# Giving all large tiles of a two-layer graph kernel one starting place modulo 256 bytes

## The chip, the cores and the metric

The kernel runs on one core of a Trainium2 chip. The metric is the device time of the whole kernel in microseconds; of several runs the median is taken.

## The reference

The input is x, 128 batches of a 128 x 512 matrix (nodes by features), in float32, and one 128 x 128 matrix adj, most of whose entries are zero. Two layers follow each other:

```python
# layer 0
h = jnp.maximum(_layernorm(x, axis=-1), 0.0)
y = jnp.einsum('nm,bmd->bnd', adj, h)
x = x + jnp.einsum('bnd,do->bno', y, weight) + bias
# layer 1
h = jnp.maximum(_layernorm(x, axis=-1), 0.0)
qkv = (h @ w_qkv)                      # 8 heads of 64
attn = q @ k^T * scale, masked where adj == 0, softmax
o = (attn @ v) @ w_proj + b_proj
x = x + o + layernorm(o) * gamma + beta
```

So each batch has one 128 x 512 by 512 x 512 product in layer 0 and four of them in layer 1 (Q, K, V and the projection), beside the small products with adj and in the attention.

## The kernel before

**Products in three parts.** Almost every large product is done with both factors split into a high and a low part, kept in the type float32r (called fp32r here; `HALF` in the code). Three sums of four matmuls, with 128 x 128 stationary and 128 x 512 moving operands, make one product: high by high, low by low, and the mixed part. `split_weights` (L333) splits the weights into `wA` (the weights of layer 0, and later the projection's), `wqk` and `wv`; `split_left` (L427) splits what comes out of PSUM into three tiles h, l and s. `times_weights` (L435, matmul on L441) does a product with the data as the stationary operand and the weights as the moving one: layer 0 (`wA` with tiles t10 to t13, t24, t25), V (`wv` with `hp`) and the projection (`wA` with t14 to t17). Q and K (L579) are the other way round: `wqk` is stationary, and `hp`, the split and transposed activations of four batches, moves. These are the fp32r products. The products with adj (L482), the scores (L636), the attention (L695) and a few plain products at the two ends (L491, L713) are in float32 and show as two records each.

**Stages.** Layer 0 (`phase1`) runs over the batches, from the fifth in pairs: load x, statistics, normalise and ReLU on ScalarE, mix with adj, split, product, add on VectorE, store twice to DRAM. Layer 1 (`phase2_group`) runs over 32 groups of four batches: fetch, normalise, transpose through DRAM (`exchange`, with `VectorE`'s 32 x 32 transposes on L542 and L677), split into `hp`, Q and K, scores, mask and softmax, V, attention, projection, second norm, store.

**Order.** A planner written in the kernel (`Plan`) gets every step with an engine, a cost, a due time and the buffers that it reads and writes, and simulates the five queues once; the instructions are then emitted in the planned order, and each engine works through its own queue. All DMAs are issued from SP's queue (L266). The planner knows buffers by name alone.

**Places in SBUF.** A tile pool stacks its tiles one after the other, in the order in which they are first made; a later tile of the same tag has the same place. Pools are stacked in the order in which they are opened. Before the change there are two in SBUF: `const` (hp, minus_half, beta_b, wA, some, maskb, means, wqk, wv, bp_b, gamma_b, in this order) and, behind it, `work`, with the t tiles (2048 bytes in each partition), the f tiles (4096 bytes) and the small m, n and l tiles (64 bytes: 16 float32 numbers, for the statistics of a normalisation or of a softmax). minus_half and some have 64 bytes as well; every other tile has a multiple of 512 bytes. The first tile, hp, begins at 128 modulo 256. The small tiles stand between the large ones, and each moves all that follow by 64 bytes. So the tiles that TensorE reads begin at these places modulo 256:

| tile | place modulo 256 |
|---|---|
| hp | 128 |
| wA | 192 |
| wqk, wv | 0 |
| t0 to t4, t8, t16, t20, t11, f0 to f3 | 0 |
| t5 to t7, t17, t9, t12, t13, t18, t19, t23 to t25 | 64 |
| t14, t15, t21, t22 | 128 |
| t10 | 192 |

Slices of these tiles begin a multiple of 512 bytes further on, so a slice has its tile's place modulo 256.

Of the kernel before, what the change touches and what calls it, by code (L numbers as in the profile page):

```python
# [15 lines left out]
P = 128  # L16
# [182 lines left out]
def kernel(  # L199
# [19 lines left out]
    assert N == P and HD * 2 == P and B % 2 == 0  # L219
    scale = HD ** -0.5  # L220

    const = ctx.enter_context(tc.tile_pool(name="const", bufs=1))
    work = ctx.enter_context(tc.tile_pool(name="work", bufs=1))
    dram = ctx.enter_context(tc.tile_pool(name="dram", bufs=B, space=bass.MemoryType.DRAM))
# [28 lines left out]
    def buf(name, shape, dtype=F32):  # L253
        if name == "ps":
            return Buf(G["ps"], lambda tag: psum.tile(shape, dtype, name=tag, tag=tag, bufs=1))
        return Buf(G[name], lambda tag: work.tile(shape, dtype, name=tag, tag=tag, bufs=1))

    def fixed(shape, name, dtype=F32):
        return Buf(None, lambda _: const.tile(shape, dtype, name=name))

    def in_dram(shape, name):
        return Buf(None, lambda _: dram.tile(shape, F32, name=name))
# [15 lines left out]


    bp_b, gamma_b, beta_b = (fixed([P, D], n) for n in ("bp_b", "gamma_b", "beta_b"))  # L280
    b0_b, junk = buf("b0", [P, D]), buf("junk", [P, D])
    adjT, maskb = buf("adjT", [P, P]), fixed([P, P], "maskb")
    minus_half = fixed([P, 16], "minus_half")
    ident = buf("ident", [P, P])
    some = fixed([P, 16], "some")

# [504 lines left out]
```

## Time and profile before

| | |
|---|---|
| median of 3 runs | 2199.84 us (2199.65 to 2200.28) |
| profiled execution | 2199.62 us, of which the span from first to last instruction is 2197.8 |
| granted TensorE clock | 0.999 of full speed |
| busy: TensorE, VectorE, ScalarE, GpSimd | 2182.2, 1717.8, 1482.1, 1524.9 us |
| fp32r matmuls | 7560: 2952 on L441 with wA, 1536 on L441 with wv, 3072 on L579 |
| DMA | 408.09 MB on SP's queue, 59.0% of the 16 engines' span |

In the profile PE is TensorE's matmuls, PEld its weight loads, which run beside them, DVE is VectorE, ACT ScalarE, POOL GpSimd and SP the queue that issues the DMAs. A line number names the line of the kernel that made the instruction. Consecutive matmuls overlap:[...] the sum of durations is more than the time that they hold TensorE, and the distance from one start to the next tells what one costs.

### The profile page before, as it was taken

To read this page: it belongs to the slowest core of one execution; us is meant where nothing else is said; L and a number is where in the kernel's file an instruction comes from. 1 tells how busy PE (TensorE), PEld (TensorE's weight loads), DVE (VectorE), ACT (ScalarE), POOL (GpSimd) and SP (SyncE) were. 2 spreads that over 40 slices of the span, in tenths; PEclk is the share of its full clock that TensorE was granted. 3 is DMA by queue.
4 is the path that set the end of the run, shared out by engine and by line. 5 is a ranking of instruction groups with operands and counts; after the bars stand their busy time and mean duration, and the time that the engine had idled before them with its cause. 6 is when DMAs were issued, how large, how long until landed. Compare 5 with 4: busy or idle time off the path is not lost.

```text
span 2197.8 us, 40584 instructions
## 1 busy us (share of the span) xinstructions
PE 2182.2 (99%) x12811; PEld 1780.3 (81%) x12811; DVE 1717.8 (78%) x3271; ACT 1482.1 (67%) x4238; POOL 1524.9 (69%) x1276
## 2 busy tenths in 40 slices
PE   9999999999999999999999999999999999999998
PEld 7888888888878888888888888888888888888885
DVE  7988887886777777777777777777777777777777
ACT  7887777767666666666666666666666666666653
POOL 6878778784667666666666666666666666666654
PEclk9999999999999999999999999999999999999999
DMA  7766666664556656655555555565555656555553
GB/s 248 237 213 223 216 212 220 227 220 153 170 169 194 183 178 184 183 180 175 173 173 173 173 175 181 178 183 182 187 180 182 186 172 193 173 175 181 176 177 119
DMA packets 297863, 410.69 MB, mean 187 GB/s; under 512 B 33072, under 2 KB 163248, under 8 KB 297648
## 3 DMA queue, kind: packets, MB, share of 16 engines
q1 hardware_dynamic: 297648, 408.09, 59.0%
q8 instruction: 102, 1.67, 0.3%
q14 instruction: 113, 0.93, 0.1%
HBM read 207.68 MB, written 200.28 MB: 186 GB/s over the span
## 4 chain that ended last, share of the span: by engine, by line
PE 92%; DVE 1%; POOL 0%; issue 0%; DMA 0%; ACT 0%; SPq 0%; POOLq 0%; DVEq 0%; ACTq 0%
PE b L441 44%; PE b L579 33%; PE b L636 6%; PE b L695 5%; PE b L482 4%; DMA out_dram<-t 0%; DVE t L729 0%; POOL f L661 0%; DVE t L727 0%; POOL m L383 0%; DVE m L377 0%; DVE t L715 0%; SPq L266 0%; ACT t L538 0%; DVE l L377 0%
## 5 line engine op out<-in xcount | busy, mean ns | idle before, releaser
L441 PE MATMUL b<-wA,t 128*128 128x512 f32 x2952 | 762.7, 397 | 1.8 <-DVE t L430 1.4
L579 PE MATMUL b<-hp,wqk 128*128 128x512 f32 x3072 | 755.9, 396 | 0.8 <-ACT t L586 0.8
L579 PEld LDWEIGHTS b<-hp,wqk 128*128 128x128 f32 x3072 | 575.6, 188 | 140.1 <-issue 4.6
L441 PEld LDWEIGHTS b<-wA,t 128*128 128x128 f32 x2952 | 545.3, 188 | 122.2 <-DVE t L430 2.4
L721 POOL TENSOR_TENSOR t<-t,t 128x512 f32<-128x512 f32 x126 | 163.9, 1301 | 446.7 <-DVE t L452 317.6
L656 ACT ACTIVATE f<-f,n 128x128 f32<-128x128 f32 x1024 | 397.1, 391 | 2.1
L441 PE MATMUL b<-wv,hp 128*128 128x512 f32 x1536 | 394.6, 398 | 0.8 <-DVE t L452 0.8
L441 PEld LDWEIGHTS b<-wv,hp 128*128 128x128 f32 x1536 | 283.6, 188 | 70.8 <-DVE t L452 1.2
L586 ACT ACTIVATE t<-b 128x512 f32<-128x512 f32 x256 | 152.4, 595 | 264.2 <-PE b L579 264.0
L644 DVE TENSOR_TENSOR f<-b,maskb 128x512 f32<-128x512 f32 x256 | 166.4, 683 | 143.4 <-PE b L695 78.3
L661 POOL TENSOR_TENSOR f<-f,n 128x1024 f32<-128x1024 f32 x128 | 245.8, 1920 | 31.4 <-DVE n L660 31.4
L429 ACT ACTIVATE t<-b 128x512 fp32r<-128x512 f32 x246 | 145.2, 590 | 111.3 <-PE b L482 87.7
L587 DVE TENSOR_TENSOR t<-b,t 128x512 f32<-128x512 f32 x256 | 172.8, 675 | 46.0 <-PE b L579 35.7
L546 POOL TENSOR_TENSOR hp<-t,hp 128x512 fp32r<-128x512 f32 x128 | 163.4, 1296 | 57.8 <-ACT hp L545 55.1
L656 ACT ACTIVATION_READ_ACCUMULATOR f<-f,n 128x1 f32 x1024 | 193.6, 189 | 0.0
L430 DVE TENSOR_TENSOR t<-b,t 128x512 fp32r<-128x512 f32 x246 | 166.9, 679 | 24.6 <-ACT t L429 24.2
L431 DVE SCALAR_TENSOR_TENSOR t<-t,b 128x512 fp32r<-128x512 f32 x246 | 166.5, 677 | 0.0
L725 POOL TENSOR_TENSOR t<-t,t 128x512 f32<-128x512 f32 x122 | 158.4, 1299 | 9.5
L549 POOL TENSOR_TENSOR hp<-hp 128x512 fp32r<-128x512 f32 x128 | 163.7, 1299 | 0.6
L724 POOL TENSOR_TENSOR t<-t,gamma_b 128x512 f32<-128x512 f32 x122 | 157.5, 1291 | 9.0 <-ACT t L723 9.0
L677 DVE STREAM_TRANSPOSE f<-f 128x1024 f32<-128x1024 f32 x126 | 155.9, 1237 | 4.0 <-DMA f<-d 3.3
L614 ACT ACTIVATE t<-b 128x512 f32<-128x512 f32 x128 | 75.8, 592 | 120.8 <-PE b L441 120.7
(119 smaller groups left out, 3204.9 us busy)
## 6 DMA issues: line engine op xcount, KB each, us to landing
d<-f SPq DMA_DIRECT2D x126, 512.0 KB, 3.3
f<-d SPq DMA_DIRECT2D x504, 128.0 KB, 4.1
t<-x1d SPq DMA_DIRECT2D x128, 256.0 KB, 4.3
d<-t SPq DMA_DIRECT2D x128, 256.0 KB, 3.0
t<-d SPq DMA_DIRECT2D x512, 64.0 KB, 3.6
t<-x1b SPq DMA_DIRECT2D x128, 256.0 KB, 3.7
out_dram<-t SPq DMA_DIRECT2D x128, 256.0 KB, 3.4
t<-in_x_dram SPq DMA_DIRECT2D x91, 256.0 KB, 3.0
```

Source lines behind the costliest of these rows:

```text
L430: op("DVE", 0.69, lambda: nc.vector.tensor_tensor(l.ap, p.ap, h.ap.bitcast(F32), op=ALU.subtract), r=[p, h], w=[l], what=name + "l")
L431: op("DVE", 0.69, lambda: nc.vector.scalar_tensor_tensor(s.ap, h.ap.bitcast(F32), UP, p.ap, op0=ALU.mult, op1=ALU.subtract), r=[p, h], w=[ ...
L441: nc.tensor.matmul(p.ap, lhsT=parts[m][2]()[:, c], rhs=w.ap[:, m, c, :], start=start and c == 0, stop=stop and c == C - 1)
L546: op("POOL", 1.35, lambda ht=ht, h=h, l=l: nc.gpsimd.tensor_tensor(l(), ht(), h().bitcast(F32), op=ALU.subtract), r=[h1, HP[i, 0]], w=[HP[ ...
L549: op("POOL", 1.38, lambda l=l, s=s: nc.gpsimd.tensor_tensor(s(), s().bitcast(F32), l().bitcast(F32), op=ALU.subtract), r=[HP[i, 1]], w=[HP ...
L579: nc.tensor.matmul(p.ap, lhsT=wqk.ap[:, which, c, col:col + P], rhs=hp[:, pick, :, which, c, :], start=start and c == 0, stop=stop and c = ...
L587: op("DVE", 0.69, lambda r=r, b=b: nc.vector.tensor_tensor(r.ap, b.ap, r.ap, op=ALU.add), r=[b], w=[r], due=tg + (4 if g < 7 else 2), what ...
L644: op("DVE", 0.68, lambda e=e, heads=heads, ps=ps: nc.vector.tensor_tensor(heads()[:, e * C:(e + 1) * C], ps[e].ap.rearrange("p c (q r) -> ...
L656: nc.scalar.activation(v[:, h], v[:, h], AF.Exp, bias=mx.ap[:, h:h + 1], scale=scale, accum_out=mx.ap[:, H + h:H + h + 1])
L661: op("POOL", 1.93, lambda heads=heads, mx=mx: nc.gpsimd.tensor_tensor(heads().rearrange("p h q r -> p q h r"), heads().rearrange("p h q r ...
L721: op(eng, us, lambda x1=x1, o=o, unit=unit: unit.tensor_tensor(x1.ap, x1.ap, o.ap, op=ALU.add), r=[o], w=[x1], due=tl + (3 if rank > 1 els ...
L725: op("POOL", 1.32, lambda x1=x1, o=o: nc.gpsimd.tensor_tensor(o.ap, o.ap, x1.ap, op=ALU.add), r=[x1], w=[o], due=tl + 9, what="out")
```

## The change

A third pool, `small`, is opened ahead of the two others, and the 13 tiles of 64 bytes are made in it: minus_half, some, m0 to m4, n0 to n3, l0 and l1. Everything else keeps its pool and its order. No instruction is added, taken away or moved.

```diff
+    small = ctx.enter_context(tc.tile_pool(name="small", bufs=1))
     const = ctx.enter_context(tc.tile_pool(name="const", bufs=1))
     work = ctx.enter_context(tc.tile_pool(name="work", bufs=1))
...
-        return Buf(G[name], lambda tag: work.tile(shape, dtype, name=tag, tag=tag, bufs=1))
+        return Buf(G[name], lambda tag: (work if tag[0] in "tf" or tag == "wA" else small).tile(shape, dtype, name=tag, tag=tag, bufs=1))
...
-        return Buf(None, lambda _: const.tile(shape, dtype, name=name))
+        return Buf(None, lambda _: (small if len(shape) == 2 and shape[1] < P else const).tile(shape, dtype, name=name))
```

`buf` gives a tile with a tag of its group (t, f, m, n, l); `fixed` gives a tile that lives through the whole kernel. Tiles whose tag begins with t or f stay in `work`, also where a t tile is only used for 16 numbers, and fixed tiles stay in `const` when their rows have 128 elements or more, as maskb and means do.

## The prediction

> **What bounds the kernel now.** I read the page's busy shares first, then its chain that ended last, then the groups, then busy time by stretches, and last the timeline of single chains of products.
>
> ```profile
> PE 2182.2 (99%) x12811; PEld 1780.3 (81%) x12811; DVE 1717.8 (78%) x3271; ACT 1482.1 (67%) x4238; POOL 1524.9 (69%) x1276
> ...
> PE 92%; DVE 1%; POOL 0%; issue 0%; DMA 0%; ACT 0%; SPq 0%; POOLq 0%; DVEq 0%; ACTq 0%
> ...
> L441 PE MATMUL b<-wA,t 128*128 128x512 f32 x2952 | 762.7, 397 | 1.8 <-DVE t L430 1.4
> L579 PE MATMUL b<-hp,wqk 128*128 128x512 f32 x3072 | 755.9, 396 | 0.8 <-ACT t L586 0.8
> ...
> L441 PE MATMUL b<-wv,hp 128*128 128x512 f32 x1536 | 394.6, 398 | 0.8 <-DVE t L452 0.8
> ```
>
> TensorE is the path: 92% of the chain, 99% busy. Three groups of fp32r products, 2952 + 3072 + 1536 = 7560, hold most of it, and they wait for other engines 3.4 us in all (last column). So the time moves only with how fast one product follows another. The mean of 397 ns is a product's latency; products overlap, so the price of one is start to start.
>
> ```profile
> 20.00:460.00 440.00, 438.01 (x2365) 372.23 (x2364) 366.19 (x823) 344.66 (x753) 351.00 (x301) 1.00 0.67 225
> ...
> 520.00:2120.00 1600.00, 1599.25 (x9667) 1299.18 (x9667) 1234.75 (x2222) 1059.60 (x3277) 1089.80 (x898) 1.00 0.58 178
> ```
>
> Columns: stretch, length, busy PE, PEld, DVE, ACT, POOL, clock, DMA share. In layer 0 the next fullest engine is DVE, 366.2 of 440 (83%); in layer 1 it is DVE again, 1234.8 of 1600 (77%). Both leave room for a TensorE that is some per cent quicker.
>
> The two chains of four below have the same line, shape, count and moving tile wA. They are the third part of a split product, of an even and of the next odd batch.
>
> ```profile
> 195.59 1.07 PE L441 MATMUL b<-wA,t 128*128 128x512 f32 x4
> ...
> 199.26 1.09 PE L441 MATMUL b<-wA,t 128*128 128x512 f32 x4
> ...
> L441 PE MATMUL b<-wA,t x4: 388/389/389, 195.6 to 196.3; 128*128 128x512 f32 x4
> ...
> L441 PE MATMUL b<-wA,t x4: 390/392/397, 199.3 to 199.9; 128*128 128x512 f32 x4
> ```
>
> The first takes (1.07 - 0.389) / 3 = 227 ns start to start, the second (1.09 - 0.397) / 3 = 231. They differ in the stationary tile: t10 against t13. By the program's list of tile places, wA begins at 192 modulo 256 bytes, t10 at 192 too, t13 at 64.
>
> I put every fp32r product of the trace, in order, beside its operands' places, took start to start within chains (7107 gaps under 260 ns, 1649.2 us, mean 232.05), and sorted by **place of the moving tile minus place of the stationary tile, modulo 256**:
>
> - 0: 191 gaps, mean 227.4 (t10 alone)
> - 64: 733 gaps, mean 231.7
> - 128: 5628 gaps, mean 232.2 (all of Q/K, where hp is at 128 and wqk at 0; all of V, where wv is at 0; wA with tiles at 64)
> - 192: 555 gaps, mean 232.3
>
> More than the means speak: at difference 128 the gaps run through a pattern, 230, 233, 241, 232, 231, 232, and the same six stand in layer 0 (wA with t12, t13) and in layer 1 (hp with wqk), on other tiles. At difference 192 the gap often sits at 233 to 234. At 0 it sits at 226, 227, 227. So the difference, not the tile, seems to set the rhythm.
>
> **What the Trainium skill says.** "SBUF — State Buffer", section "Who interferes with whom", gives TensorE separate read ports for moving operand and weights and has TensorE wait for no one; read strictly, places would not matter. The trace disagrees for this kernel: 227 against 232. The same page, "Operand start alignment", treats a start as a matter of legality and says that its runs timed nothing. "TensorE: Matmul & The Clock Gate", section "Back-to-back issue gap", has N / 2.4 + 2.5 ns, 215.8 for N = 512; the trace's least gap is 224, so some 16 of the mean 232 are not streaming, and there is something to win. "DMA: Bandwidth & Descriptors", section "How a descriptor splits into AXI transactions", charges a descriptor that starts off 256 bytes extra beats; used below.
>
> **The change part by part.**
>
> 1. *Places.* Thirteen tiles of 64 bytes (minus_half, some, five m, four n, two l) move to the front: 832 bytes. hp began at 128 modulo 256; 128 + 832 = 960 = 3 x 256 + 192. All other tiles are multiples of 512 bytes, so all begin at 192 modulo 256, moving and stationary alike; slices inside them step by multiples of 512. The sum of sizes is unchanged. No instruction, wait or order changes, since the planner knows no places; no queue (SP, POOL, others) is passed.
>
> 2. *fp32r products.* All 7107 gaps come to difference 0. Of the 62 chains on t10, 52 go straight to 226/227; ten begin otherwise (for example 233, 236, 224, or 233, 231 after a stall), mean about 231. No clean gap of the settled ones leaves the rhythm again, in some 100 steps. Chains will now be long: 100 of mean 59 gaps in layer 1, 127 of 9.5 in layer 0. I charge each of the 227 chains three gaps of 231 and the rest 226.7: 681 x 231 + 6426 x 226.7 = 1614.1 us, against 1649.2: **35.1 us less**. Bounds: nothing settles, 231 everywhere, 7.5 us less; all settle at once, 226.7 everywhere, 38 less. Below nothing: see the slower rival.
>
> 3. *Other products.* The two-pass ones (L482, L636, L695, L713) show no such dependence: scores step 7 and 105 ns with equal and with unequal places, L713 429 in all. Nothing, either way; hidden by nothing, but their 5,168 records hold still within some ns. The 234 larger gaps (79 us), where a chain begins or waits, I leave as they are.
>
> 4. *DVE, ACT, POOL.* Their rows by place: L587 681 ns at 0 and 667 at 64; L429 584 to 594; L502 1296 to 1303; L542 677 at 64 and 705 at 128. Within 5% and of both signs: counted as nothing. The cover is the 23% of DVE's time that is free in layer 1; if L542 and L677 rose 5% (254 instructions, 12 us) they would still fit.
>
> 5. *DMA.* f0 to f3, t0 to t4 and t20 leave the 256-byte boundary. By the skill's table, an estimate: 1024 bytes go from 32 beats to 38, 2048 from 64 to 70. q1's share of 59% would become about 64%. The trace speaks for less: loads of x land in 3.03 us (median of 61) at place 0 and in 2.94 (30) at 64. DVE waits 3.3 us in all for landings in L677, so cover exists; I take 0, bound 0 to 4 us lost.
>
> 6. *What is late next.* TensorE's waits are 8 us in all now; its work shrinks by 1.6%, and some producers will not keep pace at every turn (DVE at L430, ACT at L474, L586). I give back a tenth, 3 us.
>
> Sum: 35.1 - 3 = 32 less. The profiled execution took 2199.62 (span 2197.8 and 1.8 around it), within 0.01% of the median 2199.84. 2199.6 - 32 = 2167.6, said as **2168**.
>
> **The rivals.**
>
> *A: settles for good* (my forecast, 0.62): 2162 to 2178.
>
> *B: settles only in part* (0.18). For it: the ten chains at 231, of which none is seen to settle within its four. If half of the gaps stay at 231: 7107 x (232.05 - 228.85) = 23 less, 2177; if all stay, 2192. Against it: at difference 192 chains fall into 233 within a step or two of most starts seen.
>
> *C: t10's gap is its own* (0.09). One tile carries all evidence for difference 0. If something else sets its rhythm, the new places only redraw the pattern at the same mean: 2200 within 4. The skill's separate ports speak for it, the shared six-gap pattern against it.
>
> *D: slower* (0.11). The rhythm may hang on the place itself, or on the step between starts, and long chains may settle at the other steady value seen, 233.3 ns, or visit 236 more often. At 233.3 everywhere: 7107 x 1.25 = 9 more, 2209. It decides once the mean gap is over 232.05 + 4.4 / 7.107 = 232.7. For it: a steady rhythm is not a quick one, as difference 192 shows. Against it: 83% of the gaps at difference 0 are 226 or 227.
>
> *The change does not do what it says*: if the allocator rounded the small pool's end, the place would be another, but still one for all, which is the same case.
>
> **How the numbers follow.** A measurement of this kernel can tell about 0.2%, 4.4 us. Faster by more: A and B, 0.80; within: C, 0.09; slower: D, 0.11. The range goes from just under A (38 us saved and nothing given back, 2161.6) over B to the middle of C: 2161 to 2200, and leaves out D and half of C.
>
> **What would show it.** The mean start to start of L441 and L579 near 227, their latency near 389 instead of 397; TensorE still over 98% busy; the 15.05 us blocks of 64 L441 products, such as that from 870.9, at about 14.7; L482, L636 and L695 unchanged; TensorE's waits 8 to 15 us. Gaps still scattered from 228 to 241 would refute step 2; gaps at 227 with long TensorE waits would refute step 6; longer landings with DVE waiting at L677 would refute step 5.

## The result, and the profile after

The changed kernel takes 2164.78 us (median of 4 runs, 2163.97 to 2165.9) against 2200.06 for the kernel before (4 runs, 2199.65 to 2200.4). The ratio is 0.984, with a 95% interval of 0.9823 to 0.9857: 35.3 us less. The profiled execution took 2163.97, its span is 2162.2.

The page of the changed kernel, first the busy shares and the DMA queue, then the chain that ended last by engine, then the three groups of fp32r products (every line number is one higher than before, since a line was added):

```profile
PE 2147.0 (99%) x12811; PEld 1778.6 (82%) x12811; DVE 1721.4 (80%) x3271; ACT 1480.0 (68%) x4238; POOL 1524.2 (70%) x1276
...
q1 hardware_dynamic: 297648, 408.09, 62.0%
...
PE 92%; DVE 1%; POOL 0%; DMA 0%; issue 0%; ACT 0%; SPq 0%; POOLq 0%; DVEq 0%; ACTq 0%
...
L442 PE MATMUL b<-wA,t 128*128 128x512 f32 x2952 | 750.4, 393 | 2.2 <-DVE t L431 1.2
L580 PE MATMUL b<-hp,wqk 128*128 128x512 f32 x3072 | 738.8, 390 | 0.8 <-ACT t L587 0.8
...
L442 PE MATMUL b<-wv,hp 128*128 128x512 f32 x1536 | 388.2, 395 | 0.8 <-DVE t L453 0.8
```

The picture is the old one, only shorter: TensorE is still 99% busy and still 92% of the chain. Its busy time fell by 2182.2 - 2147.0 = 35.2 us, and all of that lies in three groups whose latency fell from 397, 396 and 398 ns to 393, 390 and 395. The idle time ahead of them is 3.8 us against 3.4. DVE, ACT and POOL do the same work in the same time, to within 4 us each, so their shares rose; none became a bound.

The two chains of four that the prediction compared, in the changed kernel: the timeline, and the range of their durations.

```profile
193.86 1.07 PE L442 MATMUL b<-wA,t 128*128 128x512 f32 x4
...
197.49 1.07 PE L442 MATMUL b<-wA,t 128*128 128x512 f32 x4
...
L442 PE MATMUL b<-wA,t x4: 389/389/389, 193.9 to 194.5; 128*128 128x512 f32 x4
...
L442 PE MATMUL b<-wA,t x4: 389/389/389, 197.5 to 198.2; 128*128 128x512 f32 x4
```

The chain on t13, which ran at 231 ns from start to start, now runs as the one on t10 did: (1.07 - 0.389) / 3 = 227, and every product of it has the same latency. Among the longest pieces of the chain that ended last (start, length, what) stand the same blocks as before. First two of the kernel before, then those of the changed kernel:

```profile
524.72 22.29 PE b L579 x96
870.95 15.05 PE b L441 x64
```

```profile
482.12 20.85 PE b L580 x92
519.17 21.77 PE b L580 x96
859.11 14.74 PE b L442 x64
```

The block of 64 products of V and the projection lost 0.31 / 64 = 4.8 ns a product, that of 96 products of Q and K 0.52 / 96 = 5.4 ns; the prediction had about 14.7 us for the first.

The whole span, as TensorE spends it, taken start to start from the two traces, in us:

| | before | after |
|---|---|---|
| fp32r product to fp32r product, under 260 ns | 1649.2 us, 7107 gaps of 232.05 | 1614.6 us, 7106 gaps of 227.21 |
| larger gaps and ends of fp32r chains | 139.2 | 138.4 |
| mix with adj and scores | 232.9 | 232.9 |
| attention | 123.1 | 123.1 |
| plain products at the two ends (L491, L713 before) | 34.5 | 34.5 |
| the few others (start of the kernel, transposes) | 9.7 | 9.4 |
| before the first product, after the last | 9.3 | 9.3 |

34.6 of the 35.6 us by which the spans differ lie in the first row.

### The profile page after: what moved, and what is told of

Its sections match the earlier page's. It is cut to its first block, busy times and chain, and to the rows that moved or that the text cites. A ratio compares the mean times of both kernels' runs of the same rounds, so it can differ in the third digit from the quotient of the medians.

```text
span 2162.2 us, 40584 instructions
## 1 busy us (share of the span) xinstructions
PE 2147.0 (99%) x12811; PEld 1778.6 (82%) x12811; DVE 1721.4 (80%) x3271; ACT 1480.0 (68%) x4238; POOL 1524.2 (70%) x1276
## 4 chain that ended last, share of the span: by engine, by line
PE 92%; DVE 1%; POOL 0%; DMA 0%; issue 0%; ACT 0%; SPq 0%; POOLq 0%; DVEq 0%; ACTq 0%
PE b L442 44%; PE b L580 32%; PE b L637 6%; PE b L696 5%; PE b L483 4%; DVE t L730 0%; POOL f L662 0%; DMA f<-d 0%; DVE t L728 0%; DMA out_dram<-t 0%; POOL m L384 0%; DVE m L378 0%; DVE t L716 0%; ACT t L539 0%; SPq L267 0%
## 5 line engine op out<-in xcount | busy, mean ns | idle before, releaser
L442 PE MATMUL b<-wA,t 128*128 128x512 f32 x2952 | 750.4, 393 | 2.2 <-DVE t L431 1.2
L580 PE MATMUL b<-hp,wqk 128*128 128x512 f32 x3072 | 738.8, 390 | 0.8 <-ACT t L587 0.8
L442 PE MATMUL b<-wv,hp 128*128 128x512 f32 x1536 | 388.2, 395 | 0.8 <-DVE t L453 0.8
L587 ACT ACTIVATE t<-b 128x512 f32<-128x512 f32 x256 | 151.7, 593 | 241.6 <-PE b L580 241.4
L678 DVE STREAM_TRANSPOSE f<-f 128x1024 f32<-128x1024 f32 x126 | 156.0, 1238 | 5.8 <-DMA f<-d 5.0
L650 DVE TENSOR_REDUCE n<-f 128x8 f32<-128x1024 f32 x128 | 155.1, 1212 | 1.3
```

What stands on the lines that cost most here:

```text
L442: nc.tensor.matmul(p.ap, lhsT=parts[m][2]()[:, c], rhs=w.ap[:, m, c, :], start=start and c == 0, stop=stop and c == C - 1)
L580: nc.tensor.matmul(p.ap, lhsT=wqk.ap[:, which, c, col:col + P], rhs=hp[:, pick, :, which, c, :], start=start and c == 0, stop=stop and c = ...
```

## The experiments

Theory: a product's own moving and stationary tile must begin at the same place modulo 256 bytes; then a chain of fp32r products falls into a rhythm of 226, 227, 227 ns. Rivals: the place itself is what matters; or it helps that no small tile, which other engines write, stands between the large ones; or equal places are one price and all unequal ones another. Inside a chain the product's own stationary tile and the next product's begin at the same place, so the theory leaves open which of the two counts; the section on each product's part comes back to that.

Every kernel starts from the changed one, except the last. "Apart" below means that one weight tile has a pool of its own, with small tiles ahead of it and behind it that sum to 256 bytes, so that all other large tiles stay at one place. The number in such a name is the bytes of small tiles ahead of it, not the difference; in all_at_128 and all_at_0 it is the place. The ratios are to runs of the kernel before that were taken beside each kernel (medians 2199.46 to 2200.24 us). The gaps are means start to start from the traces, in ns, over the same 7,100 or so pairs as above. The two columns of wA are parted by time, where Q and K begin; 24 late gaps of layer 0 fall into the second.

| kernel | median us | ratio to the kernel before, 95% interval | Q and K | V | wA, layer 0 | wA, projection |
|---|---|---|---|---|---|---|
| before | 2200.06 | | 232.4 | 232.3 | 231.2 | 231.9 |
| after | 2164.78 | 0.9840 (0.9823 to 0.9857) | 226.9 | 227.9 | 227.8 | 226.7 |
| all_at_128 | 2164.11 | 0.9837 (0.9820 to 0.9853) | 226.9 | 227.9 | 227.8 | 226.7 |
| all_at_0 | 2164.73 | 0.9838 (0.9823 to 0.9853) | 226.9 | 227.9 | 227.7 | 226.7 |
| wqk_256 | 2164.08 | 0.9836 (0.9822 to 0.9851) | 226.9 | 227.9 | 227.8 | 226.7 |
| wqk_128 | 2186.58 | 0.9936 (0.9921 to 0.9951) | 232.8 | 228.0 | 227.9 | 228.9 |
| wqk_64 | 2186.28 | 0.9939 (0.9922 to 0.9955) | 233.2 | 227.8 | 227.8 | 228.7 |
| wqk_192 | 2173.87 | 0.9883 (0.9868 to 0.9898) | 229.4 | 227.9 | 227.8 | 228.1 |
| wqk_32 | 2185.95 | 0.9940 (0.9925 to 0.9954) | 233.1 | 228.3 | 227.8 | 228.5 |
| wv_128 | 2174.88 | 0.9885 (0.9867 to 0.9903) | 227.1 | 231.8 | 227.8 | 229.1 |
| wA_128 | 2182.30 | 0.9921 (0.9906 to 0.9935) | 227.8 | 229.1 | 232.4 | 231.7 |
| before_qk | 2189.06 | 0.9950 (0.9935 to 0.9966) | 228.7 | 232.0 | 231.2 | 232.2 |

### Is it the place, or the difference?

**all_at_128**: the small pool stands behind all others.

```diff
-    small = ctx.enter_context(tc.tile_pool(name="small", bufs=1))
     const = ctx.enter_context(tc.tile_pool(name="const", bufs=1))
     work = ctx.enter_context(tc.tile_pool(name="work", bufs=1))
+    small = ctx.enter_context(tc.tile_pool(name="small", bufs=1))
```

> All large tiles begin at 128 modulo 256 (the small pool stands behind all others). Theory (only the difference between the moving and the stationary tile's place counts): as the changed kernel, 2163 to 2167 us, mean start to start of the fp32r products 227.2 ns. Rival 1 (the place 192 itself is the good one): well above, 2185 to 2200. Rival 2 (what helped is that no small tile, which other engines write, stands between the large ones): 2163 to 2167 as well.

Measured 2164.11 us, 227.21 ns. The place 192 has no part in it, nor have the small tiles in front.

**all_at_0**: n0, n1 and n2 in a last pool behind `work`, the other ten small tiles in front, so that hp begins at 128 + 640 = 3 x 256.

> All large tiles begin at 0 modulo 256; ten small tiles ahead, three behind. Theory (difference alone): 2163 to 2167 us, 227.2 ns. If DMAs that start off 256 bytes cost the changed kernel anything, it is gained here: SP's DMA share falls from 62% to 59 to 60%, and the time by up to 3 us; I expect the share to fall and the time to stay. Rival 1 (the place 192 is the good one): 2185 to 2200.

Measured 2164.73 us, 227.20 ns. Its DMA queue:

```profile
q1 hardware_dynamic: 297648, 408.09, 59.6%
```

The same packets and bytes took 59.6% of the engines' span, against 62.0% in the changed kernel. The loads f<-d, 1024 bytes a row, landed in 4.14 us (median of 504) against 4.37, and t<-d, 512 bytes a row, in 3.23 (median of 512) against 3.67. With all tiles at 128 the share was 60.9%, between the two. So starts off a 256-byte boundary do cost the DMA engines something, as the Trainium skill has it ("DMA: Bandwidth & Descriptors", "How a descriptor splits into AXI transactions"); here TensorE does not wait for it, and the time is the same.

### Is it the difference, or the small tiles between?

**wqk_128**: wqk apart, two n tiles ahead of it, two behind.

```diff
     const = ctx.enter_context(tc.tile_pool(name="const", bufs=1))
+    ahead, apart, behind = (ctx.enter_context(tc.tile_pool(name=n, bufs=1)) for n in ("ahead", "apart", "behind"))
     work = ctx.enter_context(tc.tile_pool(name="work", bufs=1))
...
-(work if tag[0] in "tf" or tag == "wA" else small).tile(...)
+(work if tag[0] in "tf" or tag == "wA" else ahead if tag in ['n0', 'n1'] else behind if tag in ['n2', 'n3'] else small).tile(...)
...
-(small if len(shape) == 2 and shape[1] < P else const).tile(...)
+(small if len(shape) == 2 and shape[1] < P else apart if name == "wqk" else const).tile(...)
```

> As the changed kernel, but wqk stands at 64 and all else at 192: Q and K (L580, hp moving, wqk stationary) are at difference 128 again, all other products at 0. Theory: Q and K return to 232.4 ns, 2985 gaps x 5.5 ns = 16 us more, 2181 us; V and the wA products stay at 227.9 and near 227.2. Rival 1 (place): hp stays at 192, so little moves, 2165 to 2170. Rival 2 (small tiles between): two small tiles on each side of wqk; no reason for more than 2 us, and the same for whatever number stands on each side.

**wqk_256**: the same with n0 to n3 ahead and none behind.

> Four small tiles ahead of wqk, none behind: wqk begins 256 bytes further on, so Q and K are at difference 0 modulo 256 but at 256 modulo 512. Theory (modulo 256): 2163 to 2167 us, Q and K at 226.9 ns. If the period were 512 or more: 2178 to 2184. Rival 2 (small tiles between): as wqk_128, whatever that gives.

The groups of wqk_128, and of wqk_256 behind them:

```profile
L581 PE MATMUL b<-hp,wqk 128*128 128x512 f32 x3072 | 756.5, 396 | 0.8 <-ACT t L588 0.8
L443 PE MATMUL b<-wA,t 128*128 128x512 f32 x2952 | 754.0, 394 | 3.3 <-DVE t L432 2.5 <-ACT t L431 0.4 <-DVE t L433 0.4
L443 PE MATMUL b<-wv,hp 128*128 128x512 f32 x1536 | 388.4, 395 | 0.8 <-DVE t L454 0.8
```

```profile
L443 PE MATMUL b<-wA,t 128*128 128x512 f32 x2952 | 750.3, 393 | 2.1 <-DVE t L432 1.5 <-DVE t L433 0.4 <-ACT t L431 0.2
L581 PE MATMUL b<-hp,wqk 128*128 128x512 f32 x3072 | 738.8, 390 | 0.8 <-ACT t L588 0.8
```

With 128 bytes, Q and K are back at the old latency of 396 ns, alone of the three; with 256 bytes nothing is lost. The number of small tiles is four in both. That decides for the difference modulo 256 and against the small tiles. The cost was 21.8 us where I expected 16: Q and K lost 2985 x 5.9 ns = 17.5, and the projection, whose own places are equal, lost 3.2 more. The last 1 us is not placed; TensorE's waits in the two traces differ by as much (9.5 against 7.9 us).

### How equal must the places be?

**wqk_64** (one small tile ahead, three behind), **wqk_192** (three ahead, one behind) and **wqk_32** (`some` cut to 32 bytes and put ahead; three n tiles and 32 unused bytes behind). The edit has the form of wqk_128.

> wqk at 0, all else at 192: Q and K at difference 192 (hp moving minus wqk stationary). Before, difference 192 mostly sat at 233 to 234. Theory (each difference has its own rhythm): Q and K at 233.3 ns, 2985 x 6.4 ns = 19 us, and 3 to 5 us more because the wA products that stand between them start from another rhythm, as with difference 128: 2185 to 2189 us. Rival 2 (small tiles between): as at 256 bytes, 2164.

> wqk at 128, all else at 192: Q and K at difference 64, which before had a mean of 231.7. Theory: 2985 x 4.8 ns = 14 us and 3 to 5 us from the products between: 2181 to 2184 us. Rival (only equal or unequal matters, one price for all unequal ones): as at 128, 2186.6.

> wqk at 224, all else at 192: a difference of 32 bytes, which the kernel before had nowhere. If the rhythm needs places that are equal modulo 256 exactly: 2178 to 2188, Q and K at 230 ns or more. If it follows 64-byte pieces, in which 192 and 224 are the same: 2163 to 2167. I lean to the first, without a number from before.

Moving minus stationary is 192 for wqk_64, 64 for wqk_192 and 224 for wqk_32. The Q and K group of each, in this order:

```profile
L581 PE MATMUL b<-hp,wqk 128*128 128x512 f32 x3072 | 757.7, 396 | 0.8 <-ACT t L588 0.8
```

```profile
L581 PE MATMUL b<-hp,wqk 128*128 128x512 f32 x3072 | 746.6, 393 | 0.8 <-ACT t L588 0.8
```

```profile
L582 PE MATMUL b<-hp,wqk 128*128 128x512 f32 x3072 | 757.6, 396 | 0.7 <-ACT t L589 0.7
```

32 bytes off costs as much as 128, so 64-byte pieces are not the unit. A smaller difference was not tried, nor 32 bytes the other way; 64 and 192 are also one distance with two signs, and they differ. The unequal ones have no single price: difference 64 gives 229.4 ns, and 9.1 us in all, half of what I expected from the mean of 231.7 that difference 64 had in the kernel before. There its chains were short and mixed with others. In long chains it has a rhythm of its own, such as 229, 232, 226, 229, 231, 226.

### What is each product's part?

**wv_128** and **wA_128**: wv or wA apart, two small tiles on each side, which puts it at 64.

> wv at 64, all else at 192: V (L441 with wv moving) at difference 128, everything else at 0. Theory: V from 227.9 back to 232.2 ns, 1428 x 4.3 = 6 us, and 2 to 3 us more from the projection's chains that stand between those of V and must settle again: 2172 to 2174 us. Rival (each product pays for itself alone): 2171.

> wA at 64, all else at 192: layer 0 and the projection (L441 with wA moving) at difference 128, Q, K and V at 0. Theory: layer 0 1193 gaps from 227.8 to 232, 5 us; projection 1500 gaps from 226.7 to 232.2, 8 us; and since the projection's chains of four stand between those of Q, K and V, each of these has to settle again: 2985 + 1428 gaps, some 1 to 2 ns each, 4 to 9 us. 2182 to 2187 us. Rival (each product pays for itself alone): 2178.

**before_qk**: the kernel before, with wqk alone moved to hp's place, 128, and every other large tile where it was.

```diff
+    ahead, apart, behind = (ctx.enter_context(tc.tile_pool(name=n, bufs=1)) for n in ("ahead", "apart", "behind"))
...
-lambda tag: work.tile(...)
+lambda tag: (ahead if tag in ["n0", "n1"] else behind if tag in ["n2", "n3"] else work).tile(...)
...
-lambda _: const.tile(...)
+lambda _: (apart if name == "wqk" else const).tile(...)
```

> The kernel before with one thing changed: two of the n tiles ahead of wqk and two behind it, so that wqk begins at 128, where hp begins; every other large tile keeps its old place. Q and K alone come to difference 0. Theory with settling: the projection's chains between them stay at 231.9 and unsettle Q and K each time, as in the kernel with wA apart (227.8 ns): 2985 x (232.4 - 227.8) = 14 us less, 2186 us. Rival (each product pays for itself alone): 16 to 22 us less, as much as taking Q and K apart cost, 2178 to 2184. Rival (the front pool or one common place is needed): 2200.

wA_128 came at 2182.30 us, inside what was expected; wv_128, at 2174.88, and before_qk, at 2189.06, came outside. The wA group of wA_128, then the Q and K group of before_qk:

```profile
L443 PE MATMUL b<-wA,t 128*128 128x512 f32 x2952 | 764.0, 397 | 1.8 <-DVE t L432 1.4 <-ACT t L431 0.2
```

```profile
L580 PE MATMUL b<-hp,wqk 128*128 128x512 f32 x3072 | 744.0, 392 | 0.8 <-ACT t L587 0.8
```

Taken apart one at a time, wqk costs 21.8 us, wA 17.5, wv 10.1: 49.4 in all, where all of them together cost 35.3. Put right alone, Q and K gain 11.2 (2200.24 beside it, to 2189.06), not 21.8. So a product does not pay for itself alone. The planner sets chains of four of the projection between those of Q, K and V. A chain at unequal places ends at some point of its own rhythm, and the next one needs some steps before it runs at 227. In wv_128 the projection rose from 226.7 to 229.1 though its own places are equal, and in before_qk Q and K stay at 228.7. Both were mis-sized in what I expected: 2 to 3 us for the neighbours of V, where 3.6 came from the projection, and 227.8 for Q and K.

How chains settle, counted in the trace of the changed kernel: settled means three gaps in a row of 226 or 227. Of 228 stretches of consecutive gaps 211 settle, after 2.1 steps on average in layer 0, some 5 in layer 1 and never more than 9; the 17 that don't have 2 to 10 gaps. Once settled, 5693 steps stay and none leaves. In wA_128, where chains at unequal places stand between, 174 steps leave and 2123 stay; 173 of the 174 are the first step inside a chain of the projection, to 234 or 235.

Which stationary tile counts, the product's own or the next one's? The traces tell, at the steps from one chain to another. In the changed kernel the next product's weight load begins 2 to 4 ns after a product's start (all but two of 7106 gaps) and takes 188 ns, so what is read together is this product's moving tile and the next one's stationary tile. Take all steps that follow three settled gaps, where the product's own two tiles are equal and the next product's are not:

| moving tile against the next product's stationary tile | steps | gap, ns |
|---|---|---|
| equal (wA_128, wv_128, before_qk) | 167 | 226 or 227 in 166, 232 in one |
| difference 128 (wqk_128, before_qk, before) | 40 | 232 or 233 in all |
| difference 224 (wqk_32) | 5 | 235 in all |
| difference 64 or 192 (wqk_192, wqk_64, before_qk, before) | 71 | 226 in 57, 225 in 14 |

So at these steps it is not the product's own stationary tile that sets the gap, as the theory has it, but the next one's. The same rule covers the inside of a chain. That the own tile has a part as well is not excluded, since no settled stretch is followed by a step with the own tiles unequal and the next one's equal. In wA_128 the moving tile is the odd one out, and the rhythm breaks one product later than in wqk_128, where it is the stationary tile. At differences 64 and 192 this first gap does not grow, it is even never 227, and only later gaps are long. For a kernel that gives all tiles one place, own and next are the same.

Nothing tried here says why. That the moving stream and the weight load beside it meet in the memory would fit this and a period in bytes, but no run separates it: two-pass float32 products, which also load weights, keep their 7 and 105 ns (scores) and 429 ns (L714) at equal places as at unequal ones.

## Why the prediction was right

- *Places (step 1)*: in the program's list all large tiles do begin at 192 modulo 256, with as many instructions on every engine as before.
- *fp32r products (step 2)*: 1614.1 us were worked out, 1614.6 measured. That they meet so closely is partly luck: the terms behind the sum were a little off and cancelled. Three unsettled gaps per chain were charged; it took 2.1 in layer 0 and some 5 in layer 1. And V keeps more of them than Q and K (227.9 against 226.9), since most stretches of layer 1 begin with V (66 of 100), behind the scores, and their settling falls there. The mechanism behind the step, that the difference counts and not the place, is borne out. Which stationary tile counts it did not ask; the steps from chain to chain speak for the next product's. The latencies came to 393, 390 and 395 ns and not near 389, but it is the distance from start to start that counts. The 215.8 ns that the prediction took from the Trainium skill ("TensorE: Matmul & The Clock Gate", "Back-to-back issue gap") is there the gap of an isolated matmul. The same section gives about 131 ns as sustained for N = 512; no gap of these runs comes near that, the least is 224, before and after.
- *Other products, DVE, ACT, POOL (steps 3 and 4)*: unchanged, as the table of TensorE's time and the page show. L678 takes 1238 ns where L677 took 1237, and L543 694 where L542 took 691.
- *DMA (step 5)*: q1's share rose to 62.0%, less than the 64 estimated by the skill's table, and DVE's waits for landings went from 3.3 to 5.0 us at L678 and from 3.8 to 9.9 at L543. all_at_0, with a share of 59.6% and the same time, shows that it cost nothing.
- *What is late next (step 6)*: the one term that failed. 3 us were given back for producers that would not keep pace; the fp32r groups wait 3.8 us in all against 3.4, and all waits of TensorE for other engines sum to 7.9 us against 8.4, where 8 to 15 were expected. DVE is still busy only 1237.6 of 1570 us in layer 1 (79%), and the producers that were named came late no more often than before. The forecast of 2168 is 3.2 us above the result for this reason.
- *Rivals*: B (settles in part) is refuted by the 211 of 228 stretches that settle and the 5693 steps after that without one that leaves. The ten chains that spoke for it were of four products, and settling takes up to 9 steps. D (another steady rhythm) is refuted by the rhythm itself, 226, 227, 227; C (t10's gap is its own) by every aligned kernel. The prediction set the Trainium skill's "SBUF — State Buffer", section "Who interferes with whom", against the trace. Its sentence that TensorE never waits on anyone is about other engines, and no run here shows TensorE waiting for another engine's access. But it also calls the two read ports, of the moving operand and of the weight load, independent, and for these products the measurement decides: 5 ns in 232 hang on the places of these two.

None of the aligned kernels beats the changed one: 2164.1 to 2164.8 us, within the spread of single runs.

## What to carry to other kernels

Where TensorE is the path and fp32r products follow each other closely, read start to start, not latency or busy share, and sort it by where the operands begin: a scatter that repeats on different tiles points to places. Let the moving and the stationary operands of all these products begin at the same place modulo 256 bytes. Taking the small tiles out from between the large ones does it; so does letting those between two large tiles sum to a multiple of 256 bytes, as in wqk_256. Which place it is was of no account for TensorE at 0, 128 and 192, and 0 loaded the DMA engines least. Do it for all products that interleave, since one that is off also slows those that follow it. Only products of this one shape and type were tried.

## What the runs showed of the hardware

fp32r products (128 x 128 stationary, 128 x 512 moving) with equal places settle at 226.67 ns from start to start (226, 227, 227). In the traces of all the kernels here 38,771 such steps follow a settled one, and all but three are 226 or 227 again. At the 283 steps where the two can be told apart, what counts is the moving tile's place against that of the stationary tile loaded beside it, which is the next product's. With hp moving and wqk stationary in long chains, all else equal, unequal places give 229.4 (difference 64), 232.8 (128), 233.2 (192) and 233.1 (224). The last, 32 bytes from equal, costs as much as 128; 256 costs nothing. Two-pass float32 products do not show it: in the table of TensorE's time their rows are the same before and after.
